# Layer 0's attention in one written order on four engines, the adapters' products as float32r in two parts, and the values' bias joined to the output's

## The chip, the cores and the metric

One Trainium2 chip; the kernel runs on one of its cores. The metric is the device time of one execution in microseconds (us), and lower is better. Five engines work side by side, each through a queue of its own: TensorE (PE in the profile, its weight loads PEld), VectorE (DVE), ScalarE (ACT), GpSimd (POOL) and SyncE (SP), which issues most DMAs. An instruction that waits holds up everything behind it in its engine's queue.

## The reference

Input x is 8 batches of 512 rows of 512 float32 numbers. Two layers follow each other, every half ending in a layer norm of input plus result:

```
x = layernorm(x + attention0(x))   # 16 heads of 32, causal softmax, biases on q, k, v and output
x = layernorm(x + experts(x))      # router takes 2 of 8 experts; gate_up and down each with an adapter of rank 16
x = layernorm(x + attention1(x))   # grouped heads of 64
x = layernorm(x + ffn(x))          # weights stored as integers with scales
```

The change is in the first attention and in what runs beside it. There `out = softmax(q k' / sqrt(32)) v`, and the result is `out @ WO' + bo`, with `v = x @ WV' + bv`. Each row of a softmax sums to one, so bv passes through the heads unchanged, and `bv @ WO'` may be added once to bo instead. In the experts, `W + 2 B A` may replace the weight and its adapter: the kernel adds the product B A (rank 16) to the weights in SBUF. That is called a merge here.

## The kernel before, in words

**Stages.** attention0 (L1121) runs first, over the 8 batches; the merges, the router and the first steps of the expert tiles lie in and behind it. Then come the rest of the expert tiles, attention1 and the integer FFN.

**attention0, one batch.** Heads are taken in four groups g of four (32 rows each, so that the four fill the 128 rows of TensorE). The keys are in four tiles of 128, of which only the causal part is computed. A group runs in three units u: key tile 0 (512 queries per head), tiles 1 and 3 (384 and 128), tile 2 (256). A pair (g, u) is called a slot. In each slot:

- `scores` (L1254): the score matmuls sc (L1264) into PSUM, the exp on ACT (L1268) into p, and the causal mask by selects on POOL (L1273);
- the slot's own list `todo[g, u]`, made by `plan(b)` (L1318): values (L1190), query (L1197) and key (L1205) of the next group or batch, and the pieces of the previous batch: `project` (L1213, output projection, with the layer norm L139 behind the fourth tile), `turn` (L1222, transposes of the normalised rows into x1T), `score` (L1234, router logits), `choose` (L1240), `dispatch` and `one_hot` for the batch before that (a one-hot product ps_table, L556, builds the tiles' tables in r_table), and `merge`;
- `product` (L1278) of the unit before: the matmuls av (L1288) and, on DVE, the addition of that unit's p to the group's running sum (L1296);
- in unit 1 `normalise` (L1299) of the group before: row sums rs (L1303), a copy with a check of the sums on ACT (`watch_sums`, L931), reciprocal (L1306) and product aoT (L1307) on DVE, and a check on POOL (`watch_inverses`, L934, into g_total).

The attention input x has its output bias added on POOL (L1382, one instruction for the whole batch); the values' bias is added as each ps_v is taken out of PSUM by DVE (L1195).

**Order.** `in_order(tc)` makes the scheduler keep the written order on PE, and with further arguments on other engines. Before, it holds for PE through the first unit of batch 0 (`begun`) and again from group 2 of batch 7 (`order`); in between a scheduler orders all engines, each by priority and readiness as it estimates them. DVE, ACT and POOL are in the scheduler's order all through. PSUM tiles of the pool `mm` (q, k, v, o, rs, turns, table, logits, adapters' products) share two banks.

**Merges.** 24 in all, each of two chunks of 128 x 512: `delta` (L746) is a float32 matmul of 16 rows, `merge` (L754) scales it on ACT (L760) and adds it to the weights on POOL (L762). Batches 1 to 6 hold twelve, at (2, 0) and (3, 0); two follow the last unit, ten stand between the first expert tiles' steps, one each. The adapters are loaded as 4 blocks of 16 rows for each half of the experts (`load_lora`, L740).

Of the kernel before, what the change touches and what calls it, by code (L numbers as in the profile page):

```python
# [44 lines left out]
RARE = 3  # L45
LORA = 3 * 512 + 256
EXPERT = UPS * 512

# [4 lines left out]

V_BQ, V_BK, V_NS, V_SS, V_SG, V_SU = 0, 4, 8, 12, 16, 16 + NHID
N_VEC = 16 + 2 * NHID

# [16 lines left out]
class Env:  # L73
# [53 lines left out]
    def load_adapters(self, pool):  # L127
        nc, ins = self.nc, self.ins
        self.lora_sb = pool.tile([P, 2, LORA], F32, name="lora_sb")
        for i in range(2):  # L130
            for j in range(4):
                nc.sync.dma_start(out=self.lora_sb[32 * j : 32 * j + R, i, :], in_=ins.lora[i, j])
        self.wr = pool.tile([P, ND, E], F32, name="wr")
        nc.sync.dma_start(out=self.wr, in_=ins.w_router)
        self.ra = pool.tile([R, D], F32, name="ra")
        nc.sync.dma_start(out=self.ra, in_=ins.router_lora_a)
        self.rb = pool.tile([R, E], F32, name="rb")
        nc.sync.dma_start(out=self.rb, in_=ins.router_lora_b)
# [246 lines left out]
class Router:  # L385
# [4 lines left out]
    def __init__(self, env, keep, pool, small, tmp, dram):  # L390
# [36 lines left out]
        self.tiles = numbers("r_tiles", [N_FREE], [[1, N_FREE]])  # L427
        i = tmp.tile([P, 1], I32, name="r_lane_i")
        nc.gpsimd.iota(i, pattern=[[0, 1]], base=0, channel_multiplier=1)
# [32 lines left out]
    def choose(self, b, parts, ps):  # L462
# [16 lines left out]
        nc.vector.tensor_tensor(tmp, ps, bc(red), ALU.subtract)  # L479
        nc.scalar.activation(tmp, tmp, AF.Exp)  # L480
        nc.vector.tensor_reduce(red, tmp, AX.X, ALU.add)
        nc.vector.reciprocal(red, red)
# [236 lines left out]
class Experts:  # L719
# [19 lines left out]

    def load_lora(self, pool, i):  # L740

        self.lora = pool.tile([P, LORA], F32, tag="lora", name=f"lora_{i}")
        for j in range(4):
            self.nc.sync.dma_start(out=self.lora[32 * j : 32 * j + R, :], in_=self.env.ins.lora[i, j])

    def delta(self, ps, e, c):  # L746
        j = 32 * (e % 4)
        a, bt = lora_factors(self.lora[j : j + R, :], c)
        self.nc.tensor.matmul(ps, lhsT=a, rhs=bt, start=True, stop=True)
# [15 lines left out]
class Tiles:  # L765
# [114 lines left out]

    def step(self):
        i = self.next
        self.next += 1
        if i + 1 < self.n:
            self.gate_up(i + 1, lambda: self.turn_hidden(i))
        else:
            self.turn_hidden(i)
        for n in range(4 if i == 0 else 5, 6):
            self.fetch(i + n)
        self.down(i)  # L890
        self.turn_rows(i + 3)
# [230 lines left out]
def attention0(env, guard, keep, routes, experts, dram, p_mm, tiles_ctx):  # L1122
# [8 lines left out]
    with ExitStack() as phase:  # L1131
# [32 lines left out]
        load_w(wv, 0)  # L1164
        row = work.tile([P, 2, D], F32, name="row")
        nc.sync.dma_start(out=row, in_=ins.rows.partition_broadcast(P))
        load_w(wq, 1, others)
# [7 lines left out]
        load_w(wo, 3)  # L1175
        experts.load_lora(work, 0)
        for e in range(4):
# [12 lines left out]
        def value(b, t):  # L1190
            ps = mm([P, D], "ps_v")
            for c in range(ND):
                nc.tensor.matmul(ps, lhsT=xts[b][:, c, ts(t, P)], rhs=wv[:, c, :], start=c == 0, stop=c == ND - 1)  # L1193
            vs[t] = own.tile([P, D], F32, tag=f"v{t}", name=f"v{t}")
            nc.vector.tensor_tensor(vs[t], ps, row[:, 0, :], ALU.add)  # L1195

# [16 lines left out]
        def project(b, t):  # L1213
            ps = mm([P, D], "ps_o")
            for c in range(ND):
                nc.tensor.matmul(ps, lhsT=aoTs[b][:, c, ts(t, P)], rhs=wo[:, c, :], start=c == 0, stop=c == ND - 1)  # L1216
            nc.vector.tensor_tensor(xs[b][:, t, :], ps, xs[b][:, t, :], ALU.add)
            if t == NT - 1:
                env.layernorm(b, router.rows[S * b : S * (b + 1)])

        x1Ts, logits = {}, {}

# [11 lines left out]
        def score(b):  # L1234
# [3 lines left out]
            nc.scalar.copy(logits[b], ps)  # L1238

        def choose(b):  # L1240
            router.choose(b, logits.pop(b), mm([P, NT, E], "ps_r"))

        def dispatch(b):
            router.dispatch(b, mm([P, NT, E], "ps_rank"))
# [33 lines left out]
        def product(b, g, u, p, acc):  # L1278
# [6 lines left out]
            for kt in UNITS[u]:  # L1285
                w = S - P * kt
                for j in range(4):
                    nc.tensor.matmul(av[HD * j : HD * (j + 1), P * kt :],  # L1288
                                     lhsT=vs[kt][:, P * g + HD * j : P * g + HD * (j + 1)], rhs=p[:, j, at : at + w],
                                     start=u == 0, stop=kt == UNITS[-1][-1])  # L1290
                at += w
            at = 0
            for kt in UNITS[u]:
                w = S - P * kt
                if u:
                    nc.vector.tensor_tensor(total[:, :, P * kt :], total[:, :, P * kt :], p[:, :, at : at + w], ALU.add)  # L1296
                at += w

        def normalise(b, g, acc):  # L1299
# [7 lines left out]
            nc.vector.tensor_tensor(aoTs[b][:, g, :], av, r_inv, ALU.mult)  # L1307
            guard.watch_inverses(r_inv)

        merges = [(e, c) for e in range(0, E, 2) for c in range(UPS)]  # L1310

# [6 lines left out]
        def plan(b):  # L1318
# [10 lines left out]
            if b:  # L1329
                places = ((1, 0), (1, 0), (1, 1), (1, 1) if last else (1, 2))  # L1330
                for t, slot in enumerate(places):
                    todo[slot].append(lambda t=t: project(pb, t))
                places = ((2, 0),) * 4 if last else ((2, 1), (2, 1), (2, 2), (2, 2))
                for c, slot in enumerate(places):
                    todo[slot].append(lambda c=c: turn(pb, c))
                todo[(2, 1) if last else (3, 0)].append(lambda: score(pb))
                todo[(2, 2) if last else (3, 1)].append(lambda: choose(pb))
                if not last:
                    todo[2, 0].append(merge)
                    todo[3, 0].append(merge)  # L1340
            if b == 0:
                todo[1, 0].append(lambda: router.merge_lora(mm([P, ND, E], "ps_wr")))
            if b > 1:
                todo[0, 2].append(lambda: dispatch(b - 2))
                todo[1, 1].append(lambda: enter(one_hot(b - 2, range(NT))))
            if last:
# [4 lines left out]
            return todo  # L1351

        tiles = Tiles(env, router, experts.w)

# [5 lines left out]
        def begin():  # L1360
            pair = work.tile([P, 2, D], F32, tag="row", name="first_turned")
            one = work.tile([P, S], F32, tag="logits", name="first_turned")
            tiles.begin([pair[:, 0, :], pair[:, 1, :], one], work.tile([P, 256], F32, name="first_h"),
                        lambda name: mm([P, S], name))
# [4 lines left out]
        begun = phase.enter_context(ExitStack())  # L1369
        begun.enter_context(in_order(tc))  # L1370
        query(0, 0)
        key(0, 0)
        order = phase.enter_context(ExitStack())
        waiting = summing = None
        for b in range(NB):
            todo = plan(b)
            for g in range(ND):
                if g == 2:
                    if b + 1 < NB:
                        load_xT(b + 1)  # L1380

                    nc.gpsimd.tensor_tensor(xs[b], xs[b], row[:, 1:2, :].to_broadcast([P, NT, D]), ALU.add)  # L1382
                if g == 3 and b + 1 < NB:
                    load_x(b + 1)
                if b == NB - 1 and g == 1:
                    experts.load_lora(work, 1)
                    experts.load(4)
# [6 lines left out]
                for u in range(len(UNITS)):  # L1394
                    p = scores(b, g, u)
                    for thunk in todo[g, u]:
                        thunk()
                    begun.close()
                    if waiting is not None:
                        waiting()  # L1400
                    if u == 1 and summing is not None:
                        summing()
                    waiting = lambda b=b, g=g, u=u, p=p, acc=acc: product(b, g, u, p, acc)
                summing = lambda b=b, g=g, acc=acc: normalise(b, g, acc)
        waiting()
        merge(2)
        summing()
        heads_ctx.close()
# [14 lines left out]
        for c in range(ND):  # L1423
            turn(b, c)
        tiles.step()
        score(b)
# [5 lines left out]
        for places in ((0, 1), (2, 3)):  # L1432
            rows = one_hot(b, places)
            tiles.step()
            merge()
        enter(rows)
        tiles.of_fixed = router.fixed(routes)
        while merges:
            tiles.step()
            merge()  # L1440
# [521 lines left out]
def _layout(a):  # L1962
# [26 lines left out]
    def columns(n):  # L1989
        return a[n].transpose(0, 2, 1).reshape(2, 4, R, -1)  # L1990

    lora = np.concatenate([rows("L0_ffn_gup_lora_A"), columns("L0_ffn_gup_lora_B"), columns("L0_ffn_down_lora_B"),
                           rows("L0_ffn_down_lora_A")], axis=3)
    return {
        "x": x,
# [3 lines left out]
            [cols(a[n]) for n in ("L0_attn_WQ_b", "L0_attn_WK_b", "L1_attn_norm_scale", "L1_attn_split_scale",  # L1999
                                  "L1_ffn_s_gate", "L1_ffn_s_up")], axis=1),  # L2000
        "rows": np.stack([a["L0_attn_WV_b"], a["L0_attn_WO_b"]]),
# [28 lines left out]
```

## Time and profile before

| what | value |
|---|---|
| median of 3 runs | 2297.6 us (2297.3 to 2299.71) |
| the profiled execution's own time | 2295.71 us |
| its span | 2293.9 us |
| granted TensorE clock, mean | 0.994 of full |
| PE busy | 2240.5 us (98%) |
| DVE busy | 1245.0 us (54%) |
| ACT busy | 648.2 us (28%) |
| POOL busy | 501.6 us (22%) |
| first ps_v of batches 0, 1, 2 | 15.43, 83.63, 174.37 us |
| first ps_v of batch 7; end of its last unit | 641.28; 733.58 us |

The span is the time between the first and the last instruction of one profiled execution; its own time is that run's device time, a little more. Busy times are sums over instructions. PE's end times are modelled, so "busy" says that PE had work, not that it ran at its peak. Attention0 takes about a third of the time. An engine's idle time matters only where PE waits for that engine.

### The profile page before, as it was taken

The numbers are of one execution on the slowest core, as the hardware profiler recorded it, in microseconds if no ns is written. First come the engines' busy times: TensorE is split into PE (matmuls) and PEld (weight loads), VectorE is DVE, ScalarE is ACT, GpSimd is POOL, SyncE is SP. The second block draws the span as 40 slices with busy tenths as digits, with TensorE's granted clock in tenths as the row PEclk, the third lists the DMA queues.
The fourth block names the chain that finished last, engine by engine and source line by source line (L and its number), as shares of the span: only waits on it lengthen the run. The fifth ranks groups of instructions, "written<-read, shape, count | busy, mean of one in ns | idle before, by whom it ended". The sixth has DMA issues, their size and how long they took to land.

```text
span 2293.9 us, 24187 instructions
## 1 busy us (share of the span) xinstructions
PE 2240.5 (98%) x9430; PEld 1154.8 (50%) x9430; DVE 1245.0 (54%) x1974; ACT 648.2 (28%) x937; POOL 501.6 (22%) x493
## 2 busy tenths in 40 slices
PE   9999999999999999999998999999998999999997
PEld 3344444444444444444443334443343878888876
DVE  3457575666668432242216877777667544444443
ACT  2332323323324221111223323333332322222222
POOL 2231323413224231131125122321211000000000
PEclk9999999999999999999999999999999999999999
DMA  8010110101112234332233011100100100000000
GB/s 289 19 56 1 55 33 23 56 7 49 54 38 84 92 115 146 93 120 91 87 127 94 10 55 56 55 29 17 37 1 23 42 19 19 19 19 19 19 19 20
DMA packets 58444, 126.63 MB, mean 55 GB/s; under 512 B 6210, under 2 KB 6210, under 8 KB 58322
## 3 DMA queue, kind: packets, MB, share of 16 engines
q1 hardware_dynamic: 47040, 89.32, 11.1%
q0 software_dynamic: 10560, 34.61, 5.2%
q8 instruction: 77, 1.26, 0.2%
q10 hardware_dynamic: 722, 1.07, 0.1%
q14 instruction: 45, 0.37, 0.1%
HBM read 89.59 MB, written 35.39 MB: 54 GB/s over the span
## 4 chain that ended last, share of the span: by engine, by line
PE 76%; issue 8%; DVE 7%; DMA 4%; POOL 4%; ACT 2%; POOLq 0%; SPq 0%; ACTq 0%; DVEq 0%
PE ps_f L1069 7%; PE ps_g L1055 6%; PE ps_u L1055 6%; PE ps_gu L845 5%; PE ps_o L1216 5%; PE ps_o L1551 5%; PE av L1601 5%; PE sc L1579 4%; PE ps_q L1503 4%; PE ps_q L1200 4%; PE ps_k L1208 4%; PE ps_v L1193 4%; PE av L1288 3%; PE sc L1264 3%; PE ps_y L862 2%
## 5 line engine op out<-in xcount | busy, mean ns | idle before, releaser
L845 PE MATMUL ps_gu<-experts,xrT 128*128 128x512 f32 (+1 forms) x520 | 248.6, 601 | 0.0
L1268 ACT ACTIVATE p<-sc 128x2048 f32<-128x2048 f32 (+1 forms) x96 | 152.9, 1593 | 189.0 <-PE sc L1264 182.1
L1273 POOL TENSOR_SCALAR_AFFINE_SELECT p<-p 128x512 f32<-128x512 f32 x128 | 92.1, 734 | 380.1 <-ACT p L1268 376.6
L1060 DVE SCALAR_TENSOR_TENSOR hT<-ps_u,vec,sg 128x512 f32<-128x512 f32 x88 | 65.8, 748 | 201.4 <-PE ps_u L1055 201.4
L1069 PE MATMUL ps_f<-ffn_w,h_half 128*128 128x512 f32 x672 | 169.4, 392 | 1.1 <-DVE h_half L1064 1.1
L934 POOL TENSOR_TENSOR g_total<-g_total,r_inv 128x512 f32<-128x512 f32 x64 | 89.7, 1402 | 361.4 <-DVE r_inv L1612 286.2
L1612 DVE RECIPROCAL r_inv<-r_inv 128x512 f32<-128x512 f32 x32 | 106.8, 3339 | 105.4 <-ACT r_inv L931 105.4
L1582 ACT ACTIVATE p<-sc 128x1024 f32<-128x1024 f32 x128 | 124.1, 1021 | 130.3 <-PE sc L1579 119.7
L1296 DVE TENSOR_TENSOR p<-p 128x1536 f32<-128x1536 f32 (+2 forms) x96 | 129.3, 1346 | 38.5 <-POOL p L1273 21.5
L1055 PE MATMUL ps_g<-x_high,ffn_w 128*128 128x512 f32 x352 | 141.5, 402 | 3.0 <-DVE x L1557 3.0
L1069 PEld LDWEIGHTS ps_f<-ffn_w,h_half 128*128 128x128 f32 x672 | 124.5, 188 | 33.7 <-DVE h_half L1064 7.2
L848 DVE TENSOR_TENSOR h<-ps_gu,h 128x256 f32<-128x256 f32 x67 | 28.4, 424 | 205.2 <-ACT h L847 205.2
L1055 PE MATMUL ps_g<-x_low,ffn_w 128*128 128x512 f32 x352 | 139.4, 396 | 0.0
L1055 PE MATMUL ps_u<-x_high,ffn_w 128*128 128x512 f32 x352 | 139.2, 395 | 0.0
L1055 PE MATMUL ps_u<-x_low,ffn_w 128*128 128x512 f32 x352 | 139.2, 395 | 0.0
L1579 PE MATMUL sc<-qT,kT 64*128 64x512 f32 x512 | 127.9, 618 | 1.0 <-ACT qT L1505 0.7
L862 PE MATMUL ps_y<-experts,hT 128*128 128x512 f32 (+1 forms) x272 | 127.9, 592 | 0.5 <-ACT hT L856 0.5
L1200 PE MATMUL ps_q<-experts 128*128 128x512 f32 x256 | 120.4, 611 | 4.4 <-DMA experts<-in_xT 4.4
L845 PEld LDWEIGHTS ps_gu<-experts,xrT 128*128 128x128 f32 x520 | 89.6, 192 | 68.0 <-issue 68.0
L1601 PE MATMUL av<-p,v 128*64 128x512 f32 x512 | 123.8, 605 | 0.0
L1193 PE MATMUL ps_v<-experts 128*128 128x512 f32 x256 | 116.3, 602 | 2.4 <-DVE v L1195 2.4
L1208 PE MATMUL ps_k<-experts 128*128 128x512 f32 x256 | 117.5, 602 | 0.2 <-ACT r_inv L931 0.2
(256 smaller groups left out, 3544.5 us busy)
## 6 DMA issues: line engine op xcount, KB each, us to landing
results<-y SPq DMA_DIRECT2D x68, 256.0 KB
x<-in_x SPq DMA_DIRECT2D x8, 1024.0 KB
experts<-in_gate_up SPq DMA_DIRECT2D x8, 1024.0 KB
rows<-x SPq DMA_DIRECT2D x32, 256.0 KB
x<-rows SPq DMA_DIRECT2D x8, 1024.0 KB
experts<-in_xT SPq DMA_DIRECT2D x7, 1024.0 KB
out<-x SPq DMA_DIRECT2D x28, 256.0 KB
ffn_i<-in_wq_ffn SPq DMA_DIRECT2D x11, 512.0 KB
```

The costliest lines, as they stand in the source:

```text
L845: mm = nc.tensor.matmul(ps, lhsT=xT[:, c, :], rhs=self.weights(i, c), start=c == 0, stop=c == ND - 1)
L862: self.nc.tensor.matmul(ps, lhsT=hT[:, c, :], rhs=self.weights(i, ND + c), start=c == 0, stop=c == self.NI - 1)
L1055: nc.tensor.matmul(ps, lhsT=w[:, ts(dc, P)], rhs=x[:, dc, :], start=(dc, i) == (0, 0), stop=(dc, i) == (ND - 1, 1))
L1069: self.nc.tensor.matmul(os[t], lhsT=h[:, ts(t, P)], rhs=self.weights(2 * NHID + c), start=(c, i) == (0, 0), stop=(c, i) == (NHID - 1, 1))
L1193: nc.tensor.matmul(ps, lhsT=xts[b][:, c, ts(t, P)], rhs=wv[:, c, :], start=c == 0, stop=c == ND - 1)
L1200: nc.tensor.matmul(ps, lhsT=wq[:, g, ts(c, P)], rhs=xts[b][:, c, :], start=c == 0, stop=c == ND - 1)
L1208: nc.tensor.matmul(ps, lhsT=wk[:, g, ts(c, P)], rhs=xts[b][:, c, :], start=c == 0, stop=c == ND - 1)
L1268: nc.scalar.activation(p, sc[:, :, :width], AF.Exp, scale=scale)
L1296: nc.vector.tensor_tensor(total[:, :, P * kt :], total[:, :, P * kt :], p[:, :, at : at + w], ALU.add)
L1579: nc.tensor.matmul(sc[:, j, :], lhsT=st["kT"][hs, ts(kt, P)], rhs=st["qT"][g][hs, :], start=True, stop=True)
L1582: nc.scalar.activation(p, sc, AF.Exp, scale=scale)
L1601: nc.tensor.matmul(st["av"][HD * j : HD * (j + 1), :], lhsT=st["v"][:, kt, HD * j : HD * (j + 1)], rhs=p[:, j, :], start=kt == 0, stop=kt ...
```

## The change

1. **Written order.** `begun` now holds for PE, DVE, ACT and POOL, and until batch 7. The lists are rewritten to fit: the additions of p move out of `product` into the next slot, directly behind its scores (`add`); `watch_inverses` moves one unit later; the projections stand first in slots (1, 0), (1, 1), (1, 2), (2, 0), each followed by its tile's statistics; the normalising itself (`norm`) is in (2, 2), the four turns in (3, 0), the logits in (3, 1), the choice in (3, 2) with its second half in the next batch's (0, 0); one_hot is split over (1, 2) and (2, 0) and the table product goes to (2, 2). The addition of the output bias is in four pieces, and x is loaded at (3, 1). Batch 7 keeps its places and the scheduler.
2. **Adapters.** They are stored four times over, 64 rows for an expert, and split on the chip into a part rounded to float32r (ACT) and its remainder (POOL), so that one float32r matmul of 64 rows gives the sum of the products of parts. There are 16 pieces, each fetched by a DMA of up to 256 KB: four are split in batch 0, four in batch 4, four in batch 7, four behind it. In the last loop two merges go with each step, one in the middle of it.
3. **Bias.** A ps_v is only copied now, by DVE and ACT in turn. Once, in batch 0 at (1, 2), `join_bias` multiplies bv by WO (four matmuls) and adds it to the output's bias row.

```diff
     def delta(self, ps, e, c):
-        j = 32 * (e % 4)
-        a, bt = lora_factors(self.lora[j : j + R, :], c)
+        j = P // 2 * (e % 2)
+        a, bt = lora_factors(self.lora[j : j + P // 2, :], c)
         self.nc.tensor.matmul(ps, lhsT=a, rhs=bt, start=True, stop=True)
...
+    def split_part(self, pool):
...
+        high = pool.tile([P, 512], F32R, tag="r_inv", name="l_high", bufs=2)[:, :n]
+        nc.scalar.activation(high, self.raw[:, :n], AF.Copy, scale=self.sign[:, i : i + 1])
+        raw = self.raw[:, :n]
+        nc.gpsimd.tensor_scalar(raw, raw, self.low[:, i : i + 1], None, ALU.mult)
+        nc.gpsimd.tensor_tensor(self.lora[:, at : at + n], raw, high.bitcast(F32), ALU.add)
...
+            self.fetch_part(pool)
...
-            nc.vector.tensor_tensor(vs[t], ps, row[:, 0, :], ALU.add)
+            env.evacuate(t, vs[t], ps)
+
+        def join_bias():
+
+            bv = work.tile([P, ND, P], F32, tag="r_inv", name="bv", bufs=2)
+            nc.vector.tensor_copy(bv, vec[:, V_BV : V_BV + ND, None].to_broadcast([P, ND, P]))
+            ps = mm([P, D], "ps_bias")
+            for c in range(ND):
+                nc.tensor.matmul(ps, lhsT=bv[:, c, :], rhs=wo[:, c, :], start=c == 0, stop=c == ND - 1)
+            nc.vector.tensor_tensor(row, ps, row, ALU.add)
...
+        def norm(b):
+            stats, mv, rstd = norms.pop(b)
+            for t in range(NT):
+                x = xs[b][:, t, :]
+                nc.vector.tensor_scalar(x, x, mv[:, t, 0:1], rstd[:, t, :], ALU.subtract, ALU.mult)
+                nc.sync.dma_start(out=router.rows[S * b + P * t : S * b + P * (t + 1)], in_=x)
...
-                places = ((1, 0), (1, 0), (1, 1), (1, 1) if last else (1, 2))
+                places = ((1, 0), (1, 0), (1, 1), (1, 1)) if last else ((1, 0), (1, 1), (1, 2), (2, 0))
                 for t, slot in enumerate(places):
-                    todo[slot].append(lambda t=t: project(pb, t))
-                places = ((2, 0),) * 4 if last else ((2, 1), (2, 1), (2, 2), (2, 2))
-                for c, slot in enumerate(places):
-                    todo[slot].append(lambda c=c: turn(pb, c))
-                todo[(2, 1) if last else (3, 0)].append(lambda: score(pb))
-                todo[(2, 2) if last else (3, 1)].append(lambda: choose(pb))
...
+            elif b:
+                todo[2, 2].insert(0, lambda: norm(pb))
+                todo[3, 0] += [lambda c=c: turn(pb, c) for c in range(ND)]
+                todo[3, 1].append(lambda: score(pb))
+                todo[3, 2].append(lambda: begin_choice(pb))
+                todo[2, 0].append(merge)
+                todo[3, 0].append(merge)
...
+            early = (0, 0), (0, 2), (1, 0), (1, 2)
+            slots = {0: ((2, 1), (2, 2), (3, 1), (3, 2)), 4: early, 7: early}
+            for slot in slots.get(b, ()):
+                todo[slot].append(lambda: experts.split_part(work))
             if b > 1:
+                todo[0, 0].append(lambda: end_choice(b - 2))
                 todo[0, 2].append(lambda: dispatch(b - 2))
-                todo[1, 1].append(lambda: enter(one_hot(b - 2, range(NT))))
...
-        begun.enter_context(in_order(tc))
+        begun.enter_context(in_order(tc, mybir.EngineType.DVE, mybir.EngineType.Activation, mybir.EngineType.Pool))
...
                     p = scores(b, g, u)
+                    while watches:
+                        guard.watch_inverses(watches.pop())
+                    if waiting is not None and waiting[2]:
+                        add(*waiting[2:])
                     for thunk in todo[g, u]:
                         thunk()
-                    begun.close()
                     if waiting is not None:
-                        waiting()
+                        product(*waiting)
                     if u == 1 and summing is not None:
-                        summing()
-                    waiting = lambda b=b, g=g, u=u, p=p, acc=acc: product(b, g, u, p, acc)
-                summing = lambda b=b, g=g, acc=acc: normalise(b, g, acc)
...
         while merges:
-            tiles.step()
+            tiles.step(merge)
             merge()
```

## The prediction

> **What bounds the kernel now.** I read the stretches from one first value matmul of a batch to the next, then the waits of TensorE (PE), the groups of instructions by shape, and the timeline for start-to-start times. First two of the five steady batches of layer 0's attention (columns: stretch, length, busy time of PE, its weight loads, DVE, ACT, POOL, then granted clock, DMA share, GB/s), and all PE waits from 174 to 641 us:
>
> ```profile
> 174.37:267.87 93.50, 92.33 (x481) 39.74 (x477) 61.42 (x112) 28.29 (x32) 28.98 (x27) 1.00 0.10 34
> 547.85:641.28 93.43, 92.34 (x481) 39.64 (x477) 61.83 (x112) 28.30 (x32) 28.57 (x27) 1.00 0.12 34
> ```
>
> ```profile
> PE sc L1264 <- ACT p L1268: 2.9, 5, 0.6
> PE ps_v L1193 <- DVE v L1195: 2.4, 4, 1.0
> ```
>
> PE is the bound; b2 to b6 last 466.9 us together with 5.3 us of PE idle. DVE is busy for 65%: it has room, but only where its queue's order lets it use it. So the change gains by shortening PE's list, and loses wherever PE meets something not ready. These rows price it (line, engine, operation, tiles, shapes, count, then busy us, mean ns, idle before):
>
> ```profile
> L1306 DVE RECIPROCAL r_inv<-r_inv 128x512 f32<-128x512 f32 x21 | 70.2, 3343 | 0.0
> L1296 DVE TENSOR_TENSOR p<-p 128x1536 f32<-128x1536 f32 x20 | 37.2, 1860 | 28.3 <-POOL p L1273 16.9 <-PE av L1288 11.4
> L1307 DVE TENSOR_TENSOR aoT<-av,r_inv 128x512 f32<-128x512 f32 x20 | 13.6, 682 | 3.5 <-PE ps_o L1216 3.5
> L1296 DVE TENSOR_TENSOR p<-p 128x512 f32<-128x512 f32 x20 | 12.7, 634 | 0.0
> L749 PE MATMUL ps_lora<-lora 16*128 16x512 f32 x40 | 16.3, 613 | 0.0
> ```
>
> ```profile
> L153 DVE TENSOR_SCALAR x<-x,mv,rstd x24: 545/1172/1498, 140.2 to 609.8; 128x512 f32<-128x512 f32 x24
> ```
>
> ```profile
> L1069 PE MATMUL ps_f<-ffn_w,h_half 128*128 128x512 f32 x672 | 169.4, 392 | 1.1 <-DVE h_half L1064 1.1
> ```
>
> **The steady batch (b2 to b6).** Start to start, the parts before are: 16 groups ps_q, ps_k, ps_v, ps_o of 3.53 = 56.5; sc 4 x (1.07 + 1.07 + 0.645) = 11.1; av 4 x (0.885 + 1.0 + 0.57) = 9.8; rs 4 x 0.97 = 3.9; turns 4 x 0.53 = 2.1; logits 1.0, ps_r 0.89, rank 0.46, table 1.84; two merges (pairs of ps_lora) about 1.0 each = 2.0. Together 89.6. The batch takes 93.4, so 1.06 is idle time and some 2.7 goes where single turns and merges stand between the av and sc of one unit.
>
> *Adapters.* A merge becomes two float32r matmuls of 64 rows. The integer FFN runs that type: 169.4/672 = 0.252 us each, against 0.885 for four-byte float32 of the same shape. Two can run side by side (the pairs of L749 do: 1.0 for both). A pair then costs 0.25 to 0.5; I take 0.3, by the L1069 row. Parts after: 89.6 - 2 x 0.7 = 88.2, without the 2.7, as the new list keeps the four heads' av and the turns together. Bounds: as float32 the pair keeps 1.0.
>
> *The wait at (3,0).* Slot (group, unit). Let S be the start of the scores of unit 2 in group 2. PE's list after it: sc 0.645, ps_k 3.53, table 1.84, av of unit 1 1.0, sc 1.07, so it reaches the first turn at S + 8.08. A turn needs the whole normalised x. DVE in written order: reciprocal from S + 1.02 (rs starts 0.97 before S, and the reciprocal follows rs by 1.99 in the timeline) to S + 4.36; aoT to 5.0; the adds of unit 1, 1.76 alone and 0.64, to 7.45 (7.84 if the long one takes 2.16, as beside a select); four norms at 0.54, as nothing on POOL stands beside them (its x piece ends near S + 7, the next select starts near S + 10), to 9.5 (9.8); r_table 0.84 to 10.3 (10.6); the add of unit 2 1.21 to 1.55; then the copies of the turned x, 0.68 each. So turn 0 runs at 9.5, turn 1 waits for table's bank until r_table has been read, turn 2 for the first copy (S + 12), the two deltas for the third (13.4), and the av of unit 2 ends at S + 14.6 (15.35) where S + 11.07 was free: **3.5 to 4.3 us, I take 3.9.** Behind the waiting turn stand all of PE's list; nothing passes it. Before, the same norms stood ahead of two separate turn places, and that wait is not in the list above.
>
> *Small ones.* At (2,0) both deltas share one PSUM bank, so the second waits for the first's scaled copy: +0.96. At (0,2) rank waits for v2's copy, which stands behind reciprocal, aoT and adds: +0.7 (0.5 to 0.95). Moving 16 v copies to ACT (0.68 on DVE against about 0.6 there), four x pieces of 1.13 in place of one of 4.53 on POOL, and l_high (16 of 0.6 on ACT) cost nothing on PE: ACT and POOL are busy 28 of 93 us. If that cover went, one exp late by 0.6 would cost 0.6. The 16 raw fetches of 256 KB on SP replace 8 of 16 rows; SP has nothing due in those stretches, but in b7 they stand behind the expert loads.
>
> Batch: 88.2 + 0.96 + 0.7 + 3.9 = 93.8 against 93.4; five batches: **+1.8.**
>
> **Other stretches.** b1 has no table or rank: 88.2 - 2.3 + 0.96 + 4.8 (PE comes 1.84 sooner to the same chain, table's bank being free takes some back: 4.55 to 5.1) = 91.7 against 90.74: **+0.9.** b0: four matmuls for the bias, 3.53; ps_bias waits for the bv copy, which DVE's order puts behind reciprocal, aoT and adds: ready at S + 8.1 where PE is there at S + 4.2, +3.9 to 4.3; the exps between scores in groups 1 to 3, no longer filled by half a ps_q, 0.55 + 1.46 + 1.46; less 0.35 of idle now: **+10.8.** b7 keeps its PE order: 0 (±2; split parts on ACT and POOL, fetches late on SP). The twelve merges behind the last unit: 12 x 0.75 = **-9** (-6 if pairs take 0.5, 0 if float32; +1 if an l_high waits for its fetch). Sum so far: 10.8 + 0.9 + 1.8 - 9 = **+4.5.**
>
> **The clock.** Stretches of 2 us around a cluster of PE waits late in b7:
>
> ```profile
> 718.00:720.00 2.00, 0.28 (x4) 0.29 (x8) 1.69 (x10) 1.66 (x1) 0.27 (x1) 1.00 0.89 346
> 720.00:722.00 2.00, 1.30 (x18) 0.75 (x14) 1.79 (x14) 0.99 (x1) 0.40 (x1) 0.91 0.00 0
> 722.00:724.00 2.00, 1.99 (x10) 0.90 (x14) 1.64 (x11) 0.89 (x1) 1.04 (x2) 0.50 0.03 8
> 724.00:726.00 2.00, 2.00 (x20) 0.51 (x12) 1.93 (x11) 0.22 (x1) 0.18 (x1) 0.74 0.00 0
> ```
>
> After 2.4 us of idle in 4, PE is granted half its clock for some 3.4 us. Price: 2 x (0.09 + 0.50 + 0.26) = 1.7 us. There are six such dips in the whole run (near 722, 739, 790, 801, 1220, 1776), none in b0 to b6, where no wait is over 1.0 us. They follow 0 to 4.8 us of idle; some clusters of 1 to 1.5 us, and the 5.2 us of the first 15, brought none. The change puts a cluster of 3.5 us or more into each of b0 to b6. I count half of the seven: 3.5 x 1.7 = **+6** (0 to 12).
>
> The Trainium skill ("TensorE: Matmul & The Clock Gate", "HAM oscillation — how this bites in real kernels") speaks against the change here: idle gaps above about 3.4 us bring a throttled stretch after them. By it the 3.9 us in b0 would dip, and the broken waits at (3,0), none of them above 1.3 us, would not: +1.7 in place of +6; the trace has dips after less. Its "SBUF — State Buffer" ("Who interferes with whom") says that a DVE tensor_scalar and GpSimd can lock each other out of a shared port; norm's 545 to 1498 ns agrees.
>
> **Sum:** +4.5 + 6 = +10.5. The profiled execution took 2295.7 us (span 2293.9 and 1.8 around it), 1.9 below the median of 2297.6. So 2306.2 on its scale, and **2308.1** against the median.
>
> **Rivals.**
> - *Faster: the turns are met.* If DVE's chain from reciprocal to the fourth norm fits into S + 8.08 (7.06 us from the reciprocal's start; I count 8.4 at the shortest rows), and the copies keep up, then 5 x 3.9 + 4.8 and the dips go: 10.5 - 24.3 - 6 = -19.8, 2278. For it: DVE's 35% of free time, and POOL's idle stretches. Against: each term of the chain is at its shortest row already. Half of the wait gone gives about 2293.
> - *Slower: DVE beside POOL.* If the norms take their median 1.17 in place of 0.54, each (3,0) lasts 2.5 us longer: 6 x 2.5 = +15, 2323; with a dip in each, 2329. For it: that median. Against: POOL's list.
> - *The float32r pair is not short.* At 0.5: 24 x 0.2 = +5; as float32: 24 x 0.7 = +17, 2325; the change then doesn't do what it says. For it: no row shows 64 rows in that type. Against: L1069.
>
> **Numbers.** Forecast 0.42, within 2300 to 2316; faster 0.28 (2275 to 2292); beside POOL 0.18; pair 0.12. The range 2281 to 2328 leaves out 0.1 at the faster end and 0.07 at the slower. 0.2% (4.6 us, about what a measurement of this kernel can tell from no change) puts 0.12 of the forecast's case within: faster 0.28, same 0.12, slower 0.42 - 0.12 + 0.18 + 0.12 = 0.60.
>
> **What would show it.** PE waits of 3.5 to 4.3 us per batch at ps_x1T, ps_lora and the av behind, released by norm, r_table and x1T; one near 3.9 at ps_bias, released by bv; ps_lora at 0.25 to 0.3 a pair; granted clock below 1 after those waits; a steady batch of 93 to 95 us. No such waits, or batches below 91, would prove the sum wrong; so would norms far from 0.54.

## The result, and the profile after

The changed kernel takes 2377.55 us (median of 4 runs, 2374.66 to 2378.66) against 2297.45 for the kernel before: a ratio of 1.035, 95% interval 1.033 to 1.0371. It is 80 us slower, where 10 were forecast. The profiled execution has a span of 2376.9 us and a mean granted clock of 0.974. From the page of the kernel before, then of the changed one: busy time, then PE's busy tenths (and for the changed kernel its clock) over 40 slices.

```profile
PE 2240.5 (98%) x9430; PEld 1154.8 (50%) x9430; DVE 1245.0 (54%) x1974; ACT 648.2 (28%) x937; POOL 501.6 (22%) x493
...
PE   9999999999999999999998999999998999999997
```

```profile
PE 2260.0 (95%) x9390; PEld 1165.9 (49%) x9390; DVE 1254.3 (53%) x1965; ACT 667.8 (28%) x969; POOL 541.6 (23%) x549
...
PE   8989898999989899999998999999999999999998
...
PEclk9999898999999999999999999999999999999999
```

PE has 40 matmuls fewer and yet 19.5 us more busy time: some of it ran slowly. Six of its eight slices below 9 are among the first 14, which hold attention0; the other two were low before as well. Stage by stage, in us (a batch runs from its first ps_v to the next one's; "rest" begins at the first product of the merge behind the last unit). A dip is a stretch in which the granted clock falls to half. "Clock" counts the dips and sums up, over stretches of 2 us, the length times what is missing from a clock of 1.00; a drop at the very end of every run, of 3.2 to 4.8 us, is left out. The times of proj_two to mend1 are one run each, those of mend2, mend3 and mend4 medians of 10, 4 and 10:

| kernel | time (beside it: before) | b0 | b1 | b2 to b6, mean | b7 | rest | clock: dips, us |
|---|---|---|---|---|---|---|---|
| before | 2297.45 | 68.2 | 90.7 | 93.4 | 92.3 | 1560.3 | 6, 10.2 |
| changed | 2377.55 (2297.45) | 81.1 | 103.2 | 105.8 | 90.9 | 1557.0 | 17, 56.1 |
| proj_two | 2354.49 (2293.93) | 80.4 | 96.4 | 102.3 | 90.9 | 1558.4 | 12, 35.7 |
| filled | 2367.16 (2293.93) | 80.3 | 97.6 | 105.0 | 90.9 | 1556.5 | 10, 22.1 |
| no_dve | 2297.03 (2293.93) | 76.7 | 93.8 | 92.7 | 93.5 | 1552.1 | 6, 15.3 |
| parts_2_3 | 2304.88 (2293.67) | 81.7 | 90.6 | 93.3 | 93.2 | 1554.5 | 7, 17.0 |
| only_pe | 2302.53 (2293.67) | 87.0 | 91.1 | 91.9 | 93.8 | 1552.9 | 9, 20.4 |
| bv_early | 2371.79 (2293.67) | 74.4 | 102.9 | 105.8 | 90.9 | 1557.3 | 16, 52.7 |
| mend1 | 2297.31 (2293.67) | 74.3 | 91.0 | 93.7 | 93.4 | 1553.0 | 5, 11.9 |
| mend2 | 2297.4 (2297.17) | 73.0 | 91.2 | 93.8 | 94.5 | 1552.3 | 6, 13.6 |
| mend3 | 2313.8 (2296.37) | 73.1 | 93.8 | 96.0 | 97.6 | 1553.1 | 11, 28.9 |
| mend4 | 2290.01 (2298.34) | 73.0 | 89.4 | 92.3 | 93.7 | 1550.6 | 5, 10.2 |

Of the 83.0 us between the two spans, 12.9 are in b0, 12.5 in b1, 62.3 in b2 to b6; b7 and the rest give 4.7 back.

**One batch.** b2 to b6 look alike; b1 has no rank and no table and waits 8.3 us. PE's waits in b3, in the order of time (start, us, line and tiles, then the idle time before it and its releaser):

```profile
332.01 0.41 PE L519 MATMUL ps_rank<-both,r_before 128*128 128x32 f32 x2 [0.92 <-DVE v L164]
...
366.17 0.50 PE L786 MATMUL ps_lora<-lora 64*128 64x512 f32 x1 [3.85 <-DVE x L1265]
367.42 0.79 PE L786 MATMUL ps_lora<-lora 64*128 64x512 f32 x1 [0.75 <-ACT scaled L797]
...
387.48 1.24 PE L1294 MATMUL ps_x1T<-ident,x 128*128 128x128 f32 x3 [1.26 <-DVE x L1283]
389.20 0.33 PE L1294 MATMUL ps_x1T<-ident,x 128*128 128x128 f32 x1 [0.48 <-DVE x L1283]
389.99 0.66 PE L1294 MATMUL ps_x1T<-ident,x 128*128 128x128 f32 x4 [0.46 <-DVE r_table L562]
391.72 1.97 PE L1294 MATMUL ps_x1T<-ident,x 128*128 128x128 f32 x8 [1.08 <-DVE x1T L164]
```

Together 8.8 us. The largest, 3.85, is in no step of the prediction. DVE's own timeline of the same batch shows what it is:

```profile
349.70 3.35 DVE L1384 RECIPROCAL r_inv<-r_inv 128x512 f32<-128x512 f32 x1 [1.85 <-ACT r_inv L969]
362.36 0.69 DVE L1385 TENSOR_TENSOR aoT<-av,r_inv 128x512 f32<-128x512 f32 x1 [9.31 <-PE ps_o L1264]
362.97 2.55 DVE L1374 TENSOR_TENSOR p<-p 128x1536 f32<-128x1536 f32 x2
365.43 0.69 DVE L1265 TENSOR_TENSOR x<-ps_o,x 128x512 f32<-128x512 f32 x1
```

aoT has one buffer. DVE may not write group 0 of this batch into it until the fourth projection of the batch before has read it, and that projection was moved to (2, 0). So DVE, in written order, stands for 9.3 us at an aoT that nobody needs soon (the first projection that reads it stands in the next batch), with the additions and the x that frees ps_o's PSUM bank behind it; PE wants that bank for the merge.

**The clock.** Batch b3 as one stretch (columns as in the prediction), for the changed kernel and then for mend1, an experiment below:

```profile
305.70:411.50 105.80, 96.75 (x476) 41.37 (x472) 61.08 (x110) 29.75 (x34) 27.82 (x30) 0.94 0.09 31
```

```profile
274.25:367.78 93.53, 90.08 (x476) 38.63 (x473) 61.44 (x109) 30.15 (x35) 30.06 (x30) 1.00 0.10 35
```

The same 476 matmuls keep PE busy for 96.75 us at a mean clock of 0.94 and for 90.08 at 1.00. The difference, 6.7 us, is two dips, one behind the wait at (2, 0) and one behind the waits at (3, 0). In stretches of 2 us the clock (third number from the end) goes 0.80, 0.50, 0.50, 0.50 from 366 us and 0.77, 0.50, 0.50, 0.52 from 390: 3.4 us lost in each. The first of the two:

```profile
364.00:366.00 2.00, 0.00 (x0) 0.00 (x0) 1.90 (x3) 0.00 (x0) 0.00 (x0) 1.00 0.00 0
366.00:368.00 2.00, 1.08 (x2) 0.47 (x2) 1.93 (x9) 0.60 (x1) 0.00 (x0) 0.80 0.01 4
368.00:370.00 2.00, 2.00 (x17) 0.76 (x20) 2.00 (x9) 0.60 (x1) 0.00 (x0) 0.50 0.00 0
374.00:376.00 2.00, 2.00 (x6) 0.72 (x4) 2.00 (x2) 0.00 (x0) 2.00 (x2) 1.00 0.00 0
```

A batch of the changed kernel is thus 90.2 us of PE's list, 8.8 of waits, 6.8 of clock; the same batch before was 92.3 of list and 0.6 of waits, at full clock.

### The profile page after: what moved, and what is told of

It reads as the page before. It is cut to its first block, busy times and chain, and to the rows that moved or that the text cites. A ratio compares the mean times of both kernels' runs of the same rounds, so it can differ in the third digit from the quotient of the medians.

```text
span 2376.9 us, 24225 instructions
## 1 busy us (share of the span) xinstructions
PE 2260.0 (95%) x9390; PEld 1165.9 (49%) x9390; DVE 1254.3 (53%) x1965; ACT 667.8 (28%) x969; POOL 541.6 (23%) x549
## 3 DMA queue, kind: packets, MB, share of 16 engines
q8 instruction: 77, 1.26, 0.2%
q10 hardware_dynamic: 722, 1.07, 0.1%
## 4 chain that ended last, share of the span: by engine, by line
PE 75%; DVE 10%; issue 8%; POOL 3%; DMA 3%; ACT 2%; POOLq 0%; ACTq 0%; DVEq 0%; SPq 0%
PE ps_f L1107 6%; PE ps_g L1093 6%; PE ps_u L1093 6%; PE ps_q L1248 5%; PE ps_o L1264 5%; PE av L1705 5%; PE ps_o L1655 5%; PE sc L1683 4%; PE ps_q L1607 4%; PE ps_gu L882 4%; PE ps_v L1232 4%; PE sc L1340 3%; PE av L1364 3%; PE ps_k L1256 3%; DVE p L1374 3%
## 5 line engine op out<-in xcount | busy, mean ns | idle before, releaser
L1349 POOL TENSOR_SCALAR_AFFINE_SELECT p<-p 128x512 f32<-128x512 f32 x128 | 84.0, 668 | 373.2 <-ACT p L1344 365.4
L1716 DVE RECIPROCAL r_inv<-r_inv 128x512 f32<-128x512 f32 x32 | 106.8, 3339 | 105.4 <-ACT r_inv L969 105.4
L972 POOL TENSOR_TENSOR g_total<-g_total,r_inv 128x512 f32<-128x512 f32 x64 | 83.5, 1305 | 345.4 <-DVE r_inv L1716 286.7
L1374 DVE TENSOR_TENSOR p<-p 128x1536 f32<-128x1536 f32 (+2 forms) x96 | 138.5, 1443 | 5.0 <-PE av L1364 1.9
L1384 DVE RECIPROCAL r_inv<-r_inv 128x512 f32<-128x512 f32 x32 | 107.3, 3352 | 50.9 <-ACT r_inv L969 50.9
L1248 PE MATMUL ps_q<-experts 128*128 128x512 f32 x256 | 126.8, 642 | 4.4 <-DMA experts<-in_xT 4.4
L1607 PE MATMUL ps_q<-hT,attn_qkv 128*128 128x512 f32 x256 | 117.6, 602 | 0.0
```

What stands on the lines that cost most here:

```text
L1248: nc.tensor.matmul(ps, lhsT=wq[:, g, ts(c, P)], rhs=xts[b][:, c, :], start=c == 0, stop=c == ND - 1)
L1607: nc.tensor.matmul(ps, lhsT=w_qkv[:, c, ts(g, P)], rhs=hT[:, c, :], start=c == 0, stop=c == ND - 1)
```

## The experiments

Theory A: places in DVE's written order make PE wait, and idle time brings the clock down behind it. Rivals B: the clock falls because of the float32r merges; or any written order costs.

**proj_two.**

```diff
-                places = ... else ((1, 0), (1, 1), (1, 2), (2, 0))
+                places = ... else ((1, 0), (1, 0), (1, 1), (1, 1))
```

> Changed kernel with the previous batch's four output projections back in two slots (two in (1,0), two in (1,1)), so that the last one no longer stands behind a reciprocal. Theory A (DVE's written order): aoT has one buffer, so DVE's aoT of group 0 waits at (1,2) for the fourth projection, 9.3 us, and everything behind it on DVE too; PE then waits 3.85 us at ps_lora in (2,0), and the idle time brings half a clock for about 7 us, which costs some 3.8 more. Both go: 6 x 7.6 = 46 us less, 2377 - 46 = 2331 (2325 to 2340), no ps_lora wait over 1 us, one clock dip per batch in place of two. Theory B (the clock falls because of the short float32r merges, not because of idle time): the wait of 3.85 goes, the dips stay: 2377 - 23 = 2354 (2348 to 2362), two dips per batch.

Measured: 2354.49 us, the number of B, but not for B's reason. DVE's idle time before aoT is gone and so is one dip per batch (b2 to b6 have one, of 3.4, in place of two); the waits are not gone. In b3 they sum up to 8.15 us: PE now waits for additions that stand on DVE behind one_hot, whose 12 instructions took 7.6 us:

```profile
361.00 1.06 PE L1381 MATMUL rs<-p,ones 128*32 128x512 f32 x8 [2.66 <-DVE p L1374]
363.89 3.70 PE L1256 MATMUL ps_k<-experts 128*128 128x512 f32 x8 [1.19 <-DVE q L1250]
```

The batch is 3.5 us shorter, about the one dip. A's mechanism holds for aoT; its number was wrong, as the next late thing was near.

**filled.**

```diff
+        def fill():
+            ps = p_sc.tile([P, 4, S], F32, tag="sc", name="filler")
+            for c in range(ND):
+                nc.tensor.matmul(ps[:, c, :], lhsT=wo[:, c, :P], rhs=wo[:, c, :], start=True, stop=True)
...
+                todo[2, 0].append(fill)
                 todo[2, 0].append(merge)
...
+                todo[2, 2].append(fill)
```

> Changed kernel with four float32 matmuls of 128x512 that nobody reads put in front of the merge in (2,0) and behind the table product in (2,2) of batches 1 to 6: 2 x 3.53 = 7.1 us more work per batch, in places where PE stood idle for 3.85 and 3.3 us. Theory A, with idle time as the cause of the clock's fall: the work fills the idle time and the dips (3.8 each) go: 6 x (7.1 - 7.1 - 7.6) = -46, 2331 (2325 to 2345), granted clock 1.00 in b1 to b6. More work makes it faster. Theory B (clock falls because of the merges or of the chip's power, whatever the waits): the dips stay, 2377 (2370 to 2390).

Measured: 2367.16, about 10 us less than the changed kernel with 42 us more work, and between the ranges of A and B. b1 and b2 have no dip, and b3 to b6 lose 11.9 us to dips in place of 27.2, with every merge where it was: idle time, not the merge, brings the clock down, as A has it. The waits moved here too (5.6 us in b3, 2.46 of them at ps_k for DVE's q), and so A's 2331 was missed.

**no_dve.**

```diff
-        begun.enter_context(in_order(tc, mybir.EngineType.DVE, mybir.EngineType.Activation, mybir.EngineType.Pool))
+        begun.enter_context(in_order(tc, mybir.EngineType.Activation, mybir.EngineType.Pool))
```

> Changed kernel with PE, ACT and POOL in written order in batches 0 to 6, and DVE in the scheduler's. Theory A: DVE may take the additions and x ahead of the aoT that can't start, and the norms ahead of the long additions, so both waits of PE shrink: 2377 - 55 to 75 = 2302 to 2322. Theory B (the merges, or PE's own order): nothing much changes, above 2360.

Measured: 2297.03, below A's range. It is 3.1 us above the kernel before beside it: leaving DVE out of the written order takes 77 of the 80 us away. The batches take 92.7 us with 2.1 of waits. DVE still waits for ps_o before aoT (4.86 us in b3), but the scheduler had put a reciprocal, additions and an x with its statistics ahead of it.

**no_written.** 

> Kernel before with the adapters in float32r parts and the values' bias in the output's, without the written order and the moved places. Theory A (the order costs it): the two parts alone give 24 merges shorter by some 0.7 us (-17), four more matmuls in b0 (+3.5, and a wait for bv of 0 to 4): 2282 to 2295. Theory B (float32r merges bring the clock down): dips at merges in b1 to b6, 24 x up to 2 us, above 2310.

Here the bias product had slipped into the loop over the slots of the split and is added twelve times, which changes x and the routing behind it (544 products ps_gu on xrT in place of 520). Its 2361.75 us answer nothing. It was made again as parts_2_3:

> Kernel before with the adapters in float32r parts and the values' bias in the output's, and nothing of the written order or of the moved places. Theory A (DVE's written order is what costs): 24 merges shorter by some 0.7 us (-17), four more matmuls in b0 with a wait for bv (+3.5 to 6): 2280 to 2290, steady batches of 91.5 to 92.5 us. Theory B (the float32r parts or the split cost as much as they bring): 2294 or more, steady batches of 93 or more.

Measured: 2304.88, 11 us above the kernel before, on B's side. b0 is 13.5 us longer. PE's two longest waits there are for a select on POOL and for a k on ACT. What stands ahead of these in POOL's and in ACT's queue, in the scheduler's order, is the output bias of two batches, which now has to wait for the bias product, and an l_high that waits for its fetch:

```profile
70.67 1.07 PE L1334 MATMUL av<-p,v 128*32 128x512 f32 x8 [4.07 <-POOL p L1319]
81.83 1.87 PE L1310 MATMUL sc<-q,k 32*128 32x512 f32 x8 [1.96 <-ACT k L1256]
```

```profile
61.04 8.99 POOL L1432 TENSOR_TENSOR x<-x,row 128x2048 f32<-128x2048 f32 x2
69.98 1.81 POOL L1319 TENSOR_SCALAR_AFFINE_SELECT p<-p 128x512 f32<-128x512 f32 x3
```

```profile
80.48 0.72 ACT L773 ACTIVATE l_high<-l_raw,l_sign 128x512 fp32r<-128x512 f32 x1 [4.96 <-DMA l_raw<-in_lora]
81.11 0.67 ACT L1256 ACTIVATE k<-ps_k,vec 128x512 f32<-128x512 f32 x1
```

The batches gain nothing (93.3), although a pair of products side by side takes 0.43 us where it took 1.0. The first merge stands ahead of scores that wait for an exp. In b3, first before and then here:

```profile
326.87 1.15 PE L1264 MATMUL sc<-q,k 32*128 32x384 f32 x16 [0.58 <-ACT p L1268]
341.54 1.15 PE L1310 MATMUL sc<-q,k 32*128 32x384 f32 x16 [1.00 <-ACT p L1314]
```

Of the 0.53 us that the pair saves, this wait takes 0.42 back. The second merge's two products lie apart in the scheduler's order, at 359.22 and 361.12 us, and cost 0.42 and 0.43. The stage behind the last unit ("rest") is 5.8 us shorter.

**only_pe.** The same line as in no_dve, with `in_order(tc)`.

> Changed kernel with only PE in written order in batches 0 to 6; DVE, ACT and POOL in the scheduler's. Theory A (it is DVE's order alone): the same as with DVE alone set free, 2290 to 2300, steady batches near 92.7. Rival (ACT's and POOL's orders cost too, hidden behind DVE's): below 2287, batches below 91.5.

Measured: 2302.53, slightly above A's range. Batches are 0.8 us shorter than with DVE alone set free, so ACT's and POOL's written orders cost that; but b0 is 10 us longer, with the same bunch on POOL (eight x pieces in a row, 9.84 us) ahead of a select as in parts_2_3. In b0 the written order of POOL and ACT helps.

**bv_early.** `tensor_copy(bv, ...)` in (1, 0) of batch 0, its product where it was.

> Changed kernel with the copy of bv on DVE in slot (1,0) of batch 0, ahead of the reciprocal, in place of (1,2). Theory A: PE's wait of 4.07 us at ps_bias goes, and the clock's dip behind it (0.91 and 0.91 in two stretches of 20 us) with it: 2377 - 4.1 - 1.7 to 4 = 2369 to 2372, first ps_v of b1 at 89 to 91 us in place of 96.6. Theory B (the dip has another cause): only the wait goes, 92.5 us.

Measured: 2371.79, b1 begins at 89.8 us: the wait of 4.07 and the dip behind it (3.4) are gone, as A has it.

**mend1.**

```diff
-                todo[2, 2].insert(0, lambda: norm(pb))
-                todo[3, 0] += [lambda c=c: turn(pb, c) for c in range(ND)]
-                todo[3, 1].append(lambda: score(pb))
-                todo[3, 2].append(lambda: begin_choice(pb))
+                if b > 1:
+                    todo[2, 0].append(lambda: enter(rows.pop()))
+                todo[2, 0].append(lambda: norm(pb))
+                for c, slot in enumerate(((2, 1), (2, 1), (2, 2), (2, 2))):
+                    todo[slot].append(lambda c=c: turn(pb, c))
+                todo[3, 0].append(lambda: score(pb))
+                todo[3, 1].append(lambda: begin_choice(pb))
...
-                    todo[1, 2].append(lambda: one_hot(b - 2, (0, 1)))
-                    todo[2, 0].append(lambda: rows.append(one_hot(b - 2, (2, 3))))
-                    todo[2, 2].append(lambda: enter(rows.pop()))
+                    todo[1, 0].append(lambda: one_hot(b - 2, (0, 1)))
+                    todo[1, 1].append(lambda: rows.append(one_hot(b - 2, (2, 3))))
```

> All four engines in written order, with other places: projections two in (1,0) and two in (1,1); the bv copy early; one_hot in (1,0) and (1,1) where DVE is idle; table product and norms in (2,0), ahead of the next reciprocal; turns in (2,1) and (2,2), three of their four copies on ACT; logits (3,0), choice (3,1). Theory A (it's not a written order as such, but these places in DVE's queue): PE waits below 2 us a batch, no clock dips in b1 to b6, batches of 89 to 91.5, in all 2375 - 6 x 14.5 - 6 = 2282 (2274 to 2295). Theory B (any written order holds DVE up where the scheduler wouldn't): batches above 95, 2315 or more.

Measured: 2297.31, 2 us above A's range and far below B's. All four engines stay in written order, the clock in b1 to b6 is 1.00, and 77 of the 80 us are gone (about 6 of them by bv's early copy, as in bv_early): the places were wrong, not the written order. Batches of 93.7 are 2 longer than hoped; 3.45 us of b3 are waits still.

**mend2 and mend3.** mend2: `env.evacuate(1 if t else 0, ...)` for the values, merges in (1, 2) and (3, 2), bias product in (2, 0). mend3, on top of it: the first merge in (2, 0), the table product in (2, 1), turns in (2, 2) and (3, 0), the choice in (3, 2) ahead of the merge, POOL's x pieces in groups 0 and 1.

> As mend1 (all four engines in written order), and: ps_v of tile 2 copied by ACT, which takes away rank's wait of 0.91 us; the two merges of a batch in (1,2) and (3,2), where their two products fall into different PSUM banks, which takes away 0.75 and 1.04; the bias product in (2,0) of batch 0, into a gap of 1.43 where PE waits for an exp. Theory A (PE's list bounds it once nothing in DVE's queue holds it up): batches of 93.5 - 2.7 = 90.8, b0 1.4 shorter, in all 6 x 2.7 + 1.4 = 17.6 less than mend1: 2280 (2274 to 2286), 0.5% to 0.8% below the kernel before. Theory B (the waits only move to the next thing that is late): 2288 to 2297.

Measured: 2297.4, ratio 1.000 (0.9989 to 1.001), at the upper end of B's range. The three waits went, others of the same size came (1.07 at a turn for the norms, 0.57 for an exp).

> As mend2 (all four engines in written order), and: the first merge in (2,0), between the scores of units 0 and 1 where PE waits up to 0.57 us for an exp; the table product in (2,1); turns in (2,2) and (3,0), later than the norms that they waited 1.07 us for; the four x pieces of POOL from batch 1 on in groups 0 and 1, away from DVE's norms (4.3 us for four, 2.2 without POOL beside them). Theory A (PE's list bounds it): 3.0 us of waits per batch fall to about 1, 91.2 per batch in place of 93.2, in all 6 x 2 = 12 less than mend2: 2285 (2278 to 2291). Theory B (the waits move again): 2292 to 2300.

Measured: 2313.8, worse than both theories had it. One new wait per batch, for a PSUM bank that DVE frees late, and a dip of 1.7 to 5.1 in or behind each; the row is that of b2:

```profile
275.50 0.46 PE L786 MATMUL ps_lora<-lora 64*128 64x512 f32 x1 [2.89 <-DVE tmp L481]
```

**mend4.**

```diff
-                todo[3, 2].append(lambda: begin_choice(pb))
                 todo[3, 2].append(merge)
+                todo[3, 2].append(lambda: begin_choice(pb))
```

> As mend3, but in (3,2) the merge ahead of ps_r. In mend3 a product of the merge took the PSUM bank of ps_r, which DVE frees only behind a reciprocal and the additions of p: a wait of 2.9 us per batch, and a clock dip of 1.7 to 5.1 behind it. Theory A (a wait's price is its length and the dip behind it): six waits of 2.9 and some six dips of 1.7 to 3.4 go: 2313.8 - 17 - 12 = 2285 (2279 to 2291), batches of 91 to 91.5. Theory B (the next bank is late then): 2295 to 2305.

Measured: 2290.01, ratio to before 0.9967 (0.9953 to 0.9981): two lines changed places and 23.8 us went (30.5 between the profiled spans, where waits of six times 2.9 and 18.7 us of dips are gone, which overlap in part: in mend3 the dip of b3 begins at 369.05 us, inside the wait that ends at 370.93). It is at the upper end of A's range, and faster than both kernels, than the one before by 0.33%. Its b3:

```profile
270.60:362.30 91.70, 89.75 (x476) 38.74 (x472) 60.78 (x105) 30.28 (x35) 29.75 (x30) 1.00 0.11 35
```

89.75 us of list at full clock and 1.95 of waits.

## Why the prediction was wrong

The bound was read rightly: PE's list is what counts, and PE has to find everything ready. Step by step:

- **The step that failed** is the batch's sum, "88.2 + 0.96 + 0.7 + 3.9 = 93.8". It walked (2, 0) with only the shared PSUM bank as a wait. The move of the fourth projection to (2, 0) was checked for what it issues and not for the buffer that it reads: aoT. In its place came 9.3 us of DVE, 3.85 of PE, and a dip behind it. proj_two took DVE's wait and that dip away; no_dve showed that it is the order of DVE's queue that hands it on to PE. In the sum's own terms the batch measured 90.2 of list, 8.8 of waits and 6.8 of clock: 2.0, 3.2 and 6.8 us more than the sum had.
- **The clock was mis-sized**: "I count half of the seven: 3.5 x 1.7 = +6". b0 to b6 of the changed kernel have 13 dips, of 3.4 us but for one of 5.1: 45.9 us, of which about 42 fell on work of PE, more than half of the loss. The six dips before, of 1.7 each, gave the smallest price as if it were the only one. Nor do the first 15 us show idle time without a dip, as the prediction read them: the trace's clock records begin at 8.26 us.
- The wait at (3, 0) was right: 3.3 us in four pieces against 3.9 (3.5 to 4.3), by the rows that were named (norm, r_table, x1T). So were rank (0.92 against 0.5 to 0.95), the shared bank (0.75 against 0.96) and bv (4.07 against 3.9 to 4.3). b0 came to +12.9; 3.4 of it is a dip, so the parts that the prediction added up came to 9.5 against 10.8.
- Merges: the pair side by side takes 0.43 and not 0.3. The rest is 3.3 us shorter and not 9: PE now waits 3.40 us in the merge behind the last unit for DVE's first_h, with a dip of 3.4. Without that wait (no_dve, mend1) it is 7.3 to 8.2 shorter.
- PE's list was to go from 92.3 to 88.2 and went to 90.2. The 2.7 of broken-up work did go for the most part: in mend1's b3, whose list is 90.1 at full clock, sc, av and rs take 24.9 us start to start, as the sum has it, and 27.2 in b3 before. But its two merges take 1.8 of PE's time besides their waits, where the sum had 0.6: their two products run one behind the other.
- Norms at 0.54: 2.26 us for four in b3, so the rival "DVE beside POOL" did not come here; it came in one_hot.

The Trainium skill ("TensorE: Matmul & The Clock Gate", "HAM oscillation — how this bites in real kernels") puts re-throttling at idle gaps above about 3.4 us. The 3.85 us at (2, 0) agree. The waits at (3, 0) do not: none is above 1.26 us, 3.3 in all within 5.6, and a dip follows in each of b2 to b6. The measurement decides: idle time spread over a few us is enough. Nor does a long wait always bring a dip: in proj_two's b3 0.99, 2.66 and 1.19 us within 12 us brought none, and in its b4 neither did one of 3.48 us with 1.19 behind it:

```profile
463.94 1.06 PE L1381 MATMUL rs<-p,ones 128*32 128x512 f32 x8 [3.48 <-DVE p L1374]
```

What separates these cases stands in the last section.

## What to carry to other kernels

Before an instruction is moved to a later place, list the buffers that it reads and who writes them next: with one buffer, the next writer waits, and in a queue of fixed order all behind it. Then price each wait of PE at its length plus the clock behind it, which here was between nothing and 5.1 us for waits of 2.9 to 3.9. And a wait that is taken away is worth only the distance to the next late thing: proj_two, filled and mend2 each removed waits that they named and met others.

## What the runs showed of the hardware

The clock's loss comes in steps: 1.7, 3.4 or 5.1 us, in all 110 dips of the 12 kernels' traces that are in the table. The traces' clock records show why: within a run every dip begins on one grid with a step of 3.413 us and lasts one, two or three steps at half clock. In the kernel before, dips begin at 721.64, 738.71, 789.91 and 800.15 us, which are 5, 15 and 3 steps apart.

The same grid orders the waits. I took PE's idle time (by the modelled ends of its matmuls) in each step that ran at full clock, in all 12 traces without the first 15 and the last 12 us. A dip followed all 69 steps with 1.9 us of idle or more, 25 of 42 with 1.6 to 1.9, and 16 of 7783 with less; those 16 have no explanation here. So what counts is how much idle time falls into one step, about half of it, whether in one wait or in several. The wait at (2, 0) puts 2.9 us into one step. The waits at (3, 0) put 1.6 to 1.7 into one, which is at the edge, and b2 to b6 of the changed kernel are 105.8 us long, 31 steps, so that the same work meets the same step each time: their five dips are one case and not five. proj_two's 3.48 us fell into two steps, with 1.65 and 1.84 us of idle.

A dip costs what PE has to do while it lasts. The two of 3.4 us in b3 cost nearly all of that: PE's busy time is 6.7 us longer than in mend1's b3.

DVE's one_hot instructions took 0.25 to 0.31 us alone and 1.26 to 1.35 beside POOL's additions to the weights, and to x behind them, in the same stretch of b3:

```profile
373.49 0.28 DVE L551 TENSOR_SCALAR one_hot<-r_columns,r_to_column 128x256 bf16<-128x256 bf16 x1
373.69 1.26 DVE L549 TENSOR_SCALAR one_hot<-r_columns,to_lane,r_lane 128x128 bf16<-128x128 bf16 x1
374.87 1.30 DVE L550 TENSOR_SCALAR one_hot<-r_columns,to_lane 128x128 bf16<-128x128 bf16 x1
376.09 1.35 DVE L551 TENSOR_SCALAR one_hot<-r_columns,r_to_column 128x256 bf16<-128x256 bf16 x1
```

```profile
373.56 2.56 POOL L799 TENSOR_TENSOR experts<-experts,scaled 128x512 f32<-128x512 f32 x2
376.08 1.27 POOL L1426 TENSOR_TENSOR x<-x,row 128x512 f32<-128x512 f32 x1
```

Two float32r products of 64 rows by 512 columns run side by side in 0.43 us, as in proj_two's b3, where they start at 350.50 us and the next work at 350.93. At (2, 0) in no_dve's b3, at full clock, the second waits for the scaled copy of the first (334.06, then 335.31 us, of which 0.75 are the wait), which by that releaser is put down to a shared PSUM bank; the pair takes 1.67 in all.
